# Layer 0 of a four-layer network: the wide votes' products as two operations, a new table of order, and half of the last tile's sums on VectorE

## The chip, the cores and the metric

The kernel runs on one core of a Trainium2 chip. The metric is the device time in microseconds (us) of one execution of the whole program, all four layers. Before the change the median of three runs is 6118.41 us (6118.16 to 6120.99). The engines are TensorE (PE in the profile; its weight loads are listed as PEld), VectorE (DVE), ScalarE (ACT), GpSimd (POOL) and SyncE (SP, which only issues DMAs here).

## The reference

The input `x` has shape (8, 16, 256, 256), all in float32. Four layers follow each other, each adding a function of the group-normalized input to its input. Only layer 0 is touched. It is a 3 by 3 convolution without bias whose 128 output channels are read as 8 capsules ("atoms") of 16 channels; the 8 images of the batch are the inputs between which the softmax is taken:

```
votes = conv(x, w).reshape(n, atoms, cout, h, wdt)
logits = zeros((a, b, d, e))
for _ in range(3):
    r = softmax(logits, axis=0)                       # over the 8 images
    preds = einsum('abcde,abde->bcde', votes, r)
    preds = squash(preds, axis=0)
    logits = logits + einsum('abcde,bcde->abde', votes, preds)
x = x + preds
```

`squash` scales by n2/((1+n2)·norm), where n2 is the sum of squares along the axis. In the first round the softmax is uniform, so that `preds` is a mean over the images.

## The kernel before

Layer 0 works on 64 tiles of four image rows (`TILES = H // 4`). A tile has two halves (`h` = 0 and 1) of two rows each. For each tile, `work(i)` (L505) writes down the operations:

- `prepare` (for tile i+2): fetch of `xs`, two products with `wd` that subtract means and normalize (`pd`, L487), a move on ACT (L490), and a DMA on ACT's queue that puts the rows into the scratch `d0` (L499).
- **Votes.** Half 0 goes through `votes(h, j)`, once for each row j: three fetches (`kt` in two parts, `kr`), four products with 32 rows of weights (L557), four with 128 rows (L550), two moves on ACT (L572). Half 1 goes through `wide(h)`: two fetches of 516 KB, then four calls of `votes_wide` (L579), one for each row j and each half g of the images. A call has two products with 128 rows (L587) and two with 64 rows (L591), all in one operation, and then a move on ACT (L596).
- **Squash** (L633), three times a tile: squares on ACT (L641), sums by eight small products `n` (L645), then a chain of small operations on ACT (L659 to L661), DVE (L665, L666), ACT (L670, L671) and POOL (L675 to L678) that ends in the factor `f`.
- **Logits** (L708), twice a tile: the factor is spread by four small products into `fb` (L697), DVE scales (L715) and multiplies with the votes (`pr`, L723, 2048 and 1536 elements), PE sums into `pl` (L733), ACT copies (L755 or L766), and POOL adds the older logits the second time (L760).
- **Softmax** (L771): transposes on PE (L780, L804), DVE and ACT between them.
- **Weighted** (L816), twice a tile: PE spreads the shares into `rb` and `r` (L831), DVE multiplies with the votes into `dd` (L842: per half three of 1024 elements and one of 512), and POOL adds the eight images up (L851: per half three of 512 and two of 1024 elements).
- The end: `fb` again, DVE scales (L893), POOL adds the input `res` (L896), ACT measures mean and square for the next layer (L908), SP stores.

The order in which all tiles' operations are issued is a fixed list made when the program is built. `_Order.run` (L258) ranks an operation of tile n at `n * period + TIMES[m]`, with a period of 48 and one number of `TIMES` for each operation of a tile. It always takes the lowest rank among those whose inputs exist and for which buffers are free. What is taken is appended to the queue of its engine; the engines then run their queues in order, and wait for each other by semaphores. The cost argument of `op` and its `mode` do not enter here: they belong to the search that made `TIMES`. Buffers limit how far tiles overlap: six `v` (three tiles), four `dd`, two `pr`, two `kt`, one `io` for `xs` and `res` together, and in PSUM three of `x` (for `pd`, `cv`, `fb`, `rb`) and two of `u` (for `n`, `pl`, `lg`, `rt`, `r`).

PE is used in four shapes in this layer: 128 rows by 128 columns of weights (L487, L550, L587, L780, L804), 64 rows (L591, L697), 32 rows (L557, L831), and 128 rows by 32 columns (L645, L733).

Of the kernel before, what the change touches and what calls it, by code (L numbers as in the profile page):

```python
# [12 lines left out]
ALU = mybir.AluOpType  # L13
# [10 lines left out]
TILES = H // 4  # L24
# [160 lines left out]
class _Buf:  # L185
# [10 lines left out]


TIMES = [
    -1017.19, 743.46, 708.62, 498.18, -984.65, -996.51, -997.22, 751.01, 751.99, 751.01, 752.12, 750.77,
    -967.35, -903.62, -974.59, 753.99, 754.00, 753.77, 445.66, 393.73, -780.66, -960.80, 755.37, 755.59, 760.20,  # L200
    707.64, 775.69, 780.13, 782.25, 565.91, 658.76, 763.54, 681.24, 605.08, 709.84, 767.15, 644.09, 776.33,
    664.78, 790.04, 756.59, 796.59, 757.08, 765.74, 797.09, 318.31, 799.87, 800.80, 377.30, 696.72, 800.88,
    717.59, 571.56, 737.04, 802.63, 604.46, 530.71, 804.53, 784.88, 636.95, 657.50, 800.06, 517.07, 807.24,
    715.03, 742.15, 830.33, 840.65, 809.85, 812.29, 605.85, 802.98, 816.03, 807.95, 821.83, 824.88, 831.28,
    830.39, 840.66, 789.85, 845.72, 805.49, 748.11, 612.37, 736.06, 636.75, 809.44, 848.88, 838.39, 852.49,
    854.69, 850.98, 859.07, 855.18, 468.16, 857.49, 859.83, 859.02, 698.63, 610.89, 868.22, 704.59, 653.78,
    580.88, 884.00, 654.67, 695.12, 888.80, 889.83, 889.82, 808.47, 890.27, 690.66, 805.44, 696.48, 782.31,
    896.59, 899.53, 896.48, 777.07, 667.15, 682.59, 886.03, 640.00, 674.37, 898.75, 899.76, 887.82, 843.57,
    670.73, 902.64, 828.29, 828.95, 658.08, 885.55, 571.52, 801.95, -872.70, 907.37, 403.39, 814.67, 908.69,
    735.69, 919.60, 844.76, 829.08, -789.01  # L210
]


# [79 lines left out]
class _Net:  # L293
# [123 lines left out]
    def layer0(self, wd, bd, less0, tiles=range(TILES)):  # L417
# [5 lines left out]
        nc, tc = self.nc, self.tc  # L423
        xf = self.d["x"].rearrange("b c h w -> (b c) (h w)")
        last = B - 1
        with ExitStack() as st:
# [6 lines left out]
            w = w0[:, : 2 * P].rearrange("p (s m) -> p s m", s=2)  # L433
# [12 lines left out]
            for i in range(2):  # L446
                t = one.tile([P, 4, WP], F32, name=f"dn{i}")
                nc.vector.memset(t, 0.0)
                ring.append(t)
            for row in (0, H + 1):  # L450
                nc.sync.dma_start(
                    out=self.d0[row * ROW : row * ROW + ROW].rearrange("(p w) -> p w", p=P), in_=ring[0][:, 0, :]
                )
                nc.sync.dma_start(
                    out=self.x1[row and 15, :, :, row and 9, row and 1, :].rearrange("b c w -> (b c) w"),
# [3 lines left out]
                    out=self.x1p[:, row and 1, :, row and H // 2, :], in_=ring[0][:, 0, 0:W]  # L459
# [7 lines left out]
            def buf(kind, shape, name=None):  # L467
                pool = psum if kind in banks else sbuf
                n = {**places, **banks}[kind]
                return _Buf(kind, lambda: pool.tile(shape, F32, name=name or kind, tag=kind, bufs=n))  # L470
# [34 lines left out]
            def work(i):  # L505
# [3 lines left out]
                def op(*a, **k):  # L509
                    ops.append(order.op(*a, **k))  # L510
# [7 lines left out]
                v = [buf("v", [P, 8, 512]) for _ in range(2)]  # L518
# [60 lines left out]
                def votes_wide(h, kt, j, g):  # L579

                    ps = buf("x", [P, 2, 512], "cv")

                    def products():
                        t = kt().rearrange("p (a w) -> p a w", a=8)
                        for n in range(2):
                            a = 4 * g + 2 * n
                            nc.tensor.matmul(ps()[:, n], w2[:, 0, j, :], t[:, a : a + 2, 0:W], start=True, stop=False)  # L587
                        for n in range(2):
                            a = 4 * g + 2 * n
                            at = slice(n * 64, n * 64 + 64)  # L590
                            nc.tensor.matmul(  # L591
                                ps()[:, n], w2[at, 1, j, :], t[at, a : a + 2, 2 - n : 2 - n + W], start=False, stop=True
                            )

                    def move():
                        nc.scalar.copy(  # L596
                            v[h]()[:, 4 * g : 4 * g + 4, j * W : j * W + W],
                            ps().rearrange("p n (a w) -> p (n a) w", w=W),
                        )

                    op("PE", 3.2, products, [(kt, 0), (kt, 1)], [(ps, 0), (v[h], "turn")], mode="votes")
                    op("ACT", 1.1, move, [(ps, 0)], [(v[h], g, j)])

                def wide(h):
                    kt = buf("kt", [P, 8 * WP])
                    for dx in range(2):

                        def fetch(dx=dx):
                            at = (4 * i + 2 * h) * ROW + dx
                            nc.sync.dma_start(  # L610
                                out=kt()[dx * 64 : dx * 64 + 64],
                                in_=self.d0[at : at + 4 * ROW].rearrange("(p f) -> p f", f=8 * WP),
                            )

                        op("SP", 0.5, fetch, [("d0", i), ("d0", i + 2 * h - 1)], [(kt, dx)], lag=6.0)
                    for g in (1, 0):
                        for j in range(2):
                            votes_wide(h, kt, j, g)

                def voted(h, a):  # L620
                    return [(v[h], a // 4, 0), (v[h], a // 4, 1)]
# [8 lines left out]
                def rows(ap):  # L630
                    return ap.rearrange("p (r w) -> p r w", w=W)
# [184 lines left out]
                def weighted(rs):  # L816


                    s = buf("s", [P, 2, 2, W])
                    for h in range(2):  # L820

                        def term(images, h=h):

                            rb = [buf("x", [P, 2, 512], "rb") if len(a) == 2 else buf("u", [P, 1, 512], "r6") for a in images]

                            def products():
                                for pair, r in zip(images, rb):
                                    for n, a in enumerate(pair):
                                        g, j = a // 4, (0, 2, 1, 3)[a % 4]
                                        at = slice(32 * j, 32 * j + 32)  # L830
                                        nc.tensor.matmul(  # L831
                                            r()[:, n], spread[at, g, h, :], rs()[at], start=True, stop=True
                                        )

                            op("PE", 1.25, products, [(rs, 0)], [(r, 0) for r in rb] + [(s, "turn")], mode="r32")
                            out = []
                            for pair, r in zip(images, rb):
                                n, a = len(pair), pair[0]
                                dd = buf("dd", [P, 2, 512])

                                def multiply(n=n, a=a, r=r, dd=dd):
                                    nc.vector.scalar_tensor_tensor(  # L842
                                        dd()[:, :n], r()[:, :n], 1.0 / B, v[h]()[:, a : a + n], ALU.subtract, ALU.mult
                                    )

                                op("DVE", 0.2 + 0.52 * n, multiply, [(r, 0)] + voted(h, a), [(dd, 0)])
                                out.append(dd)
                            return out

                        def add(out, a, b, us):  # L850
                            op("POOL", us, lambda: nc.gpsimd.tensor_tensor(out[0](), a[0](), b[0](), ALU.add),  # L851
                               a[1] + b[1], out[1])

                        d45, d6 = term([(4, 5), (6,)])
                        sh = (lambda h=h: s()[:, :, h], [(s, h)])
                        add(
                            sh,
                            (lambda h=h: rows(v[h]()[:, last]), voted(h, last)),
                            (lambda d=d6: rows(d()[:, 0]), [(d6, 0)]),
                            1.3,  # L860
                        )
                        d01, d23 = term([(0, 1), (2, 3)])
                        both = (d01, [(d01, 0)])
                        add(both, both, (d45, [(d45, 0)]), 2.4)
                        add(both, both, (d23, [(d23, 0)]), 2.4)
                        for n in range(2):
                            add(sh, sh, (lambda d=d01, n=n: rows(d()[:, n]), [(d01, 0)]), 1.3)
                    return s
# [7 lines left out]
                for _ in range(2):  # L876
                    ls = logits(s, read, f, before)
                    before = ls
                    t = weighted(softmax(ls))
# [1043 lines left out]
```

## Time and profile before

| what | value |
|---|---|
| median of three runs | 6118.41 us |
| profiled execution | 6118.06 us, span of its instructions 6116.3 us |
| layer 0, from the first `pd` product to the start of its closing statistics | 101.0 to 3275.8 us |
| from one place in a tile to the same place in the next, in the steady part | 47.59 us |
| PE busy, whole span | 5816.4 us (95%) |
| DVE, POOL, ACT busy, whole span | 85%, 63%, 53% |

In these tables a float32 product of 512 columns shows as two records of PE, and a transpose as one. A line of the timeline has a start, the busy time from first start to last end, the engine, the line of the code, the operation, its output and inputs, the sizes, and the count. A line of the chain of waits has a start, a length and what it is; the chain is followed back from the last instruction to whatever released it. "issue" in the chain is time in which nothing that the profile shows was waited for.

### The profile page before, as it was taken

The page shows a single profiled execution, that of the slowest core. Times are in us where ns is not written, and L with a number is a line of the kernel's source. Part 1 is how long each engine was busy: PE and PEld are TensorE (multiplying, and loading weights), DVE is VectorE, ACT ScalarE, POOL GpSimd, SP SyncE. Part 2 cuts the span into 40 slices and gives each one's busy share as a digit, 9 for nine tenths or more (in the row PEclk, how much of TensorE's full clock was granted, in tenths as well). Part 3 has the DMA queues.
Part 4 walks back from the last instruction along what each step waited for, and adds up shares of the span by engine and source line. Part 5 has one row for each costly group of instructions (what it writes and reads, how often), then busy time and mean ns, then how long its engine had stood idle before and what let it go on. Part 6 is the DMA issues. An engine that isn't in the chain of part 4 may idle for free.

```text
span 6116.3 us, 118361 instructions
## 1 busy us (share of the span) xinstructions
PE 5816.4 (95%) x46024; PEld 2945.8 (48%) x46024; DVE 5191.8 (85%) x6933; ACT 3236.8 (53%) x4986; POOL 3828.0 (63%) x3679
## 2 busy tenths in 40 slices
PE   2999999999999999999985999999999999999998
PEld 0344444444444444444432444444444589999853
DVE  5799999999999999999986999999999777777741
ACT  0444454444544445444435888888888533333321
POOL 0588888888888888888884444444443344444333
PEclk9999999999999999999997999999999999999999
DMA  7455555555555555555524555555556554445458
GB/s 291 114 141 136 128 138 143 137 136 128 143 141 136 132 131 144 141 136 129 136 75 132 186 184 179 181 179 179 181 182 177 155 101 102 96 89 103 115 179 265
DMA packets 599967, 902.55 MB, mean 148 GB/s; under 512 B 294130, under 2 KB 370514, under 8 KB 572402
## 3 DMA queue, kind: packets, MB, share of 16 engines
q1 hardware_dynamic: 555570, 831.70, 50.3%
q10 hardware_dynamic: 33984, 34.08, 1.8%
q0 software_dynamic: 9856, 29.20, 1.7%
q8 instruction: 367, 6.01, 0.4%
q14 instruction: 190, 1.56, 0.1%
HBM read 684.09 MB, written 210.77 MB: 146 GB/s over the span
## 4 chain that ended last, share of the span: by engine, by line
PE 80%; DVE 7%; issue 5%; POOL 4%; DMA 2%; ACT 2%; SPq 0%; DVEq 0%; POOLq 0%; ACTq 0%
PE ps L1123 23%; PE rb L831 8%; PE cv L587 7%; PE pq L1539 6%; PE pl L733 6%; PE cv L591 4%; PE cv L550 4%; PE psc L1607 4%; PE po L1623 4%; PE p L1740 3%; PE pv L1539 3%; DVE pr L723 2%; PE fb L697 2%; PE pd L487 2%; PE cv L557 1%
## 5 line engine op out<-in xcount | busy, mean ns | idle before, releaser
L1123 PE MATMUL ps<-bases,tw 128*32 128x512 f32 (+1 forms) x13824 | 1340.5, 545 | 13.3 <-POOL bases L1089 13.3
L851 POOL TENSOR_TENSOR dd<-dd 128x1024 f32<-128x1024 f32 x512 | 1212.0, 2367 | 70.0 <-DVE dd L842 64.8
L723 DVE TENSOR_TENSOR pr<-v,fb 128x2048 f32<-128x2048 f32 (+1 forms) x512 | 1020.7, 2014 | 17.0 <-PE pl L733 12.5
L1123 PEld LDWEIGHTS ps<-bases,tw 128*32 128x32 f32 x13824 | 620.4, 109 | 753.6 <-issue 477.3
L842 DVE SCALAR_TENSOR_TENSOR dd<-rb,v 128x1024 f32<-128x1024 f32 x768 | 906.7, 1214 | 8.8 <-POOL dd L851 3.3
L851 POOL TENSOR_TENSOR s<-s,dd 128x512 f32<-128x512 f32 x512 | 647.7, 1275 | 15.1
L1089 POOL TENSOR_TENSOR bases<-e,a 128x1024 f32<-128x1024 f32 (+1 forms) x264 | 615.9, 2354 | 12.5 <-DVE e L1082 12.2
L831 PE MATMUL rb<-rs,ct_fold 32*128 32x512 f32 x3072 | 593.0, 634 | 25.6 <-DVE pr L723 20.1
L1093 POOL COPY mark<-e 128x1 f32<-128x1 f32 x127 | 23.6, 186 | 865.3 <-DVE e L1061 857.4
L851 POOL TENSOR_TENSOR s<-v,dd 128x512 f32<-128x512 f32 x256 | 329.0, 1285 | 290.5 <-DVE dd L842 290.5
L587 PE MATMUL cv<-kt,w 128*128 128x512 f32 x1024 | 497.3, 608 | 11.8 <-DMA kt<-d 10.6
L733 PE MATMUL pl<-pr,ct_fold 128*32 128x512 f32 x3584 | 505.1, 601 | 3.0 <-DVE pr L723 3.0
L550 PE MATMUL cv<-kt,w 128*128 128x512 f32 x1024 | 477.3, 609 | 4.8 <-DMA kt<-d 4.8
L596 ACT COPY v<-cv 128x1024 f32<-128x1024 f32 x256 | 251.9, 1008 | 303.8 <-PE cv L591 303.8
L1637 POOL COPY y<-y 128x2 f32<-128x2 f32 x128 | 24.1, 189 | 599.5 <-DVE y L1628 599.5
L831 PEld LDWEIGHTS rb<-rs,ct_fold 32*128 32x128 f32 x3072 | 226.1, 185 | 325.3 <-issue 129.0
L697 PEld LDWEIGHTS fb<-f,ct_fold 64*128 64x128 f32 x3072 | 208.2, 188 | 310.2 <-issue 176.2
L1069 ACT ACTIVATE sq<-a 128x1024 f32<-128x1024 f32 (+1 forms) x264 | 263.9, 999 | 148.1 <-DVE a L1061 142.1
L842 DVE SCALAR_TENSOR_TENSOR dd<-r,v 128x512 f32<-128x512 f32 x256 | 177.0, 692 | 190.5 <-PE r L831 175.9
L572 ACT COPY v<-cv 128x1024 f32<-128x1024 f32 x256 | 258.2, 1009 | 139.2 <-PE cv L550 139.1
L550 PEld LDWEIGHTS cv<-kt,w 128*128 128x128 f32 x1024 | 184.7, 190 | 289.8 <-issue 283.0
L1082 DVE TENSOR_TENSOR a<-a,sq 128x1024 f32<-128x1024 f32 (+1 forms) x264 | 313.6, 1188 | 9.4 <-ACT sq L1069 9.4
(323 smaller groups left out, 11753.9 us busy)
## 6 DMA issues: line engine op xcount, KB each, us to landing
kt<-d SPq DMA_DIRECT2D x256, 387.0 KB
kt<-d SPq DMA_DIRECT2D x128, 516.0 KB
xr<-x1p SPq DMA_DIRECT2D x128, 512.0 KB
xt<-x1p SPq DMA_DIRECT2D x120, 512.0 KB
d<-dn ACTq DMA_DIRECT2D x64, 516.0 KB
kr<-d SPq DMA_DIRECT2D x128, 258.0 KB
kt<-d SPq DMA_DIRECT2D x128, 258.0 KB
x<-y SPq DMA_DIRECT2D x128, 258.0 KB
```

The source lines that it names most:

```text
L550: nc.tensor.matmul(ps[g]()[:, n], w[:, 0], t[:, a : a + 2, 0:W], start=False, stop=True)
L587: nc.tensor.matmul(ps()[:, n], w2[:, 0, j, :], t[:, a : a + 2, 0:W], start=True, stop=False)
L697: nc.tensor.matmul(fb()[:, j, n * P : n * P + P], unfold[at, h, n, :], f()[at, 3], start=True, stop=True,)
L723: nc.vector.tensor_tensor(pr()[:, :n].rearrange("p n (r w) -> p n r w", w=W), v[h]()[:, 4 * g : 4 * g + n].rearrange("p n (r w) -> p n r w ...
L733: nc.tensor.matmul(pl()[at : at + 32], sel[:, g, h, :], pr()[:, t, :], start=h == 0 and g == 0, stop=h == 1 and (g == 1 or t == 3),)
L831: nc.tensor.matmul(r()[:, n], spread[at, g, h, :], rs()[at], start=True, stop=True)
L842: nc.vector.scalar_tensor_tensor(dd()[:, :n], r()[:, :n], 1.0 / B, v[h]()[:, a : a + n], ALU.subtract, ALU.mult)
L851: op("POOL", us, lambda: nc.gpsimd.tensor_tensor(out[0](), a[0](), b[0](), ALU.add), a[1] + b[1], out[1])
L1082: nc.vector.tensor_tensor(q, q, part[4 + k], ALU.mult)
L1089: nc.gpsimd.tensor_tensor(ring[n % 3][:, 0, p : p + m, 1 : 1 + W], rows(e), rows(a), ALU.subtract)
L1123: nc.tensor.matmul(out if k is None else out[:, k], lhs, rhs, start=start, stop=stop, skip_group_check=True)
L1539: nc.tensor.matmul(out, lhs, rhs, start=start, stop=stop, skip_group_check=True)
```

## The change

It has three parts. `products()` of `votes_wide` becomes two operations, `most` (the two products with 128 rows) and `rest` (the two with 64 rows), each placed by the order on its own. `TIMES` has one number more for each of the four wide calls of a tile, and all its numbers are new. In the last tile (`i == TILES - 1`) the ten additions of half 1 (five in each of the two weighted sums) go to DVE; all others stay on POOL. The amount of arithmetic is the same.

```diff
@@ -196,18 +196,19 @@
 TIMES = [
-    -1017.19, 743.46, 708.62, 498.18, -984.65, -996.51, -997.22, 751.01, 751.99, 751.01, 752.12, 750.77,
...
+    788.93, 1208.48, 1101.33, 1188.73, -10349.17, -10412.56, -10390.23, 1181.37, 1174.54, 1141.94, 1180.94,
...
 ]
@@ -580,11 +581,14 @@
                     ps = buf("x", [P, 2, 512], "cv")
 
-                    def products():
+                    def most():
                         t = kt().rearrange("p (a w) -> p a w", a=8)
                         for n in range(2):
                             a = 4 * g + 2 * n
                             nc.tensor.matmul(ps()[:, n], w2[:, 0, j, :], t[:, a : a + 2, 0:W], start=True, stop=False)
+
+                    def rest():
+                        t = kt().rearrange("p (a w) -> p a w", a=8)
                         for n in range(2):
                             a = 4 * g + 2 * n
                             at = slice(n * 64, n * 64 + 64)
@@ -598,7 +602,8 @@
-                    op("PE", 3.2, products, [(kt, 0), (kt, 1)], [(ps, 0), (v[h], "turn")], mode="votes")
+                    op("PE", 1.8, most, [(kt, 0), (kt, 1)], [(ps, 0), (v[h], "turn")], mode="votes")
+                    op("PE", 1.0, rest, [(kt, 0), (kt, 1)], [(ps, 0)], mode="r64")
                     op("ACT", 1.1, move, [(ps, 0)], [(v[h], g, j)])
@@ -847,8 +852,10 @@
-                        def add(out, a, b, us):
-                            op("POOL", us, lambda: nc.gpsimd.tensor_tensor(out[0](), a[0](), b[0](), ALU.add),
+                        name, engine = ("DVE", nc.vector) if h and i == TILES - 1 else ("POOL", nc.gpsimd)
+
+                        def add(out, a, b, us, name=name, engine=engine):
+                            op(name, us, lambda: engine.tensor_tensor(out[0](), a[0](), b[0](), ALU.add),
                                a[1] + b[1], out[1])
```

## The prediction

> **What bounds the kernel now.** I read the busy time by stretches first: what limits layer 0, and where that stops.
>
> ```profile
> core 0: us, PE busy (x) PEld busy (x) DVE busy (x) ACT busy (x) POOL busy (x), PEclk, DMA share, GB/s
> 1973.00:2020.60 47.60, 46.91 (x294) 19.39 (x293) 43.38 (x48) 23.44 (x44) 42.16 (x36) 1.00 0.54 136
> 3164.00:3290.00 126.00, 56.71 (x334) 24.30 (x334) 70.03 (x107) 31.08 (x68) 81.14 (x73) 0.65 0.20 64
> ```
>
> In a steady tile (47.6 us) PE is busy 46.9, DVE 43.4, POOL 42.2: PE bounds, and two engines are 10% behind it, so that a short delay soon shows. In the tail (second row) no engine is full, POOL leads, and the granted clock is 0.65. Next the chain of waits inside one tile, for what a product, a change of shape and a wait cost:
>
> ```profile
> 2029.76 3.63 PE cv L550 x8
> 2033.39 0.60 PE rt L804 x4
> 2033.99 1.72 PE cv L587 x4
> 2035.71 1.06 PE cv L591 x4
> ...
> 2039.06 0.57 PE n L645 x16
> 2039.64 0.86 PE pl L733 x8
> 2040.49 0.65 PE fb L697 x8
> 2041.14 1.91 PE cv L587 x4
> ...
> 2047.89 0.69 DVE s L893
> 2048.66 1.27 POOL s L896
> 2049.93 1.24 POOL ls L760
> ```
>
> Four records of L587 take 1.72 after `rt`, which has their shape: 0.43 each. After `fb` (64 rows) they take 1.91, and L550 takes 3.63 for eight where 3.44 is due: **a change to a shape of 128 columns costs 0.19 to 0.20.** `n` and `pl` share a shape, so `pl` is 0.86 clean; `n` is 0.57 for 0.44 of work, so a change to 32 columns costs 0.13. The last rows are a wait: PE's `lg` stands behind POOL's `ls`, which stands behind an addition of the input. Then the tail, on POOL:
>
> ```profile
> 3247.17 4.77 POOL L851 TENSOR_TENSOR dd<-dd 128x1024 f32<-128x1024 f32 x2 [0.99 <-DVE dd L842]
> 3251.90 1.26 POOL L851 TENSOR_TENSOR s<-v,dd 128x512 f32<-128x512 f32 x1
> 3260.29 2.60 POOL L851 TENSOR_TENSOR s<-s,dd 128x512 f32<-128x512 f32 x2
> ```
>
> The last tile's last sums keep POOL busy without a break from 3247.17 to 3262.89, and layer 0 ends on them.
>
> **Steady part: work of PE.** Write F for 128x128, H for 64 rows, Q for 32 rows, C for 32 columns. From one `pd` to the next, PE's old order is F Q C H C Q F Q C H F Q F H Q C H F H Q C H C H Q F H F H: 29 changes, 6 of them to C. The changed program has F H F H Q H C Q F Q C H F Q F C H F H C Q C Q C F H F Q C: 29 again, 7 to C. So the split saves no change of shape: three of the four wide calls stay in one piece, and in the fourth the transposes `rt` (F) stand between the parts. 1 x (0.195 - 0.13) is a gain of 0.07. All products are the same: 36 full passes (15.5), 8 pairs of 64-row passes (3.4), 32-row groups (1.7 for votes, 6.9 for `rb`), `pl` 6.9, the small ones 5.7, together 40.1; with 23 x 0.195 + 6 x 0.13 = 5.3 this is 45.4 of the 47.59. **The other 2.2 are waits**, and they decide.
>
> **Steady part: waits.** I laid both orders out side by side over a tile, each instruction with the duration of its row (DVE: `pr` 2.28 and 1.75, `dd` 1.21 and 0.69, 0.08 less when the next follows at once; POOL: 2.37, 1.28, four steps of `f` 1.66; ACT: move 1.01, square 0.63), and with the gaps that the rows show between an end and what waits for it (0.05 to PE, 0.2 from PE's last start plus 0.43, 0.08 between dependent additions on POOL). For the old order that gives these waits of PE: second pair of `rb` 0.42 and 0.39 (bank still read by DVE's `pr` or `dd`), `rb` after L550 0.36, `lg` on ACT's copy 0.13, second pair of L557 0.24, `rt` and the product after it 0.22, `rb` 0.10, `lg` on POOL's `ls` 0.39, small ones 0.06: 2.31, which with the work comes within 0.1 of the measured 47.59. For the new order:
>
> - Gone: `lg` on `ls` (0.39), one of the two `rb` waits (0.4), `rt` (0.2), `rb` (0.1): 1.1.
> - Kept: `rb` after L550 0.38, `lg` 0.13, L557 0.24: the same.
> - **Second pair of `rb`, 0.65 in place of 0.42.** It needs the bank of `fb`. From the start of that `fb`: 0.76 to the scale, 0.69, then `pr` 2.28 and 1.75, 5.55 with the gaps. On PE only `fb`, `rt`, one wide call and half the `rb` lie between, 4.9.
> - **Second half of `n`, 0.36, new.** A 64-row half, then `lg`, four `rb` and half of `n` on PE, 2.05; against 0.2, the move 0.91, squares 0.53 and 0.63, 0.05 on ACT, 2.32; plus the weights that are then loaded in the open.
> - **`fb` on `f`, 0.28, new.** POOL has two additions of `dd`, three of `s` and the four steps of `f` in a row before it; dependent ones follow at 0.08 apart instead of overlapping by 0.04.
> - **A wide call on a bank of `dd` 0.26, `fb` on a bank of `pr` 0.20, small ones 0.10**, all new.
>
> The sum is 0.75 + 0.65 + 0.36 + 0.28 + 0.26 + 0.20 + 0.10 = 2.60. So a tile changes by 2.60 - 2.31 - 0.07 = **+0.22 to +0.24**; over some 60 tiles after the start and before the tail, **+14**. Bounds: each of the new waits is known to perhaps 0.05, and the old order was missed by up to 0.1; from 0 a tile (the lost waits outweigh: 0) to +0.42 (+25). If POOL's run of additions had more cover, `fb` would not wait; if it has less, what is late next is DVE's `pr`, then the `rb` behind it.
>
> **Fetches.** The number of DMAs is the same. In the trace a `kt` lands 6.3 to 6.6 after issue (up to 9.1), and PE waited for one in only 9 cases, 6.8 in all. The new order has the same two `kt` buffers to fetch ahead into. 0, bounds -4 to +7.
>
> **Start.** SP's queue now has tile 1's `xs` behind eight fetches of tile 0's votes, which wait for `d0` (landed at 110.1). They carry 2.6 MB, 11 us at the 239 GB/s that the stretch from 113 to 129 us shows: `xs` lands near 125 to 128, and PE, where `pd` of tile 1 stands ahead of the votes, waits for it (before: votes at 120.1). But the wide products could not start before 147.5 anyhow, since their fetch took 15.8 beside others; the later one finds fewer beside it (6.6 in the steady part). +1, bounds -4 to +8.
>
> **Tail.** Half 1's additions, 2 x 1.21 + 3 x 0.69 = 4.5 on DVE by layer 1's sums of that shape and `s`-sized rows, run beside half 0's 8.6 on POOL. The last sums would end near 3258 instead of 3262.9, and those of the round before gain about 3. Against it: on ACT the four measuring operations of tile 62 (0.8 each) now stand ahead of the inverse of tile 63's last squash, and wait for tile 62's last addition: +4. Together **-3**, bounds -8 to +3.
>
> Here a rule speaks against the change. The layer 1 rows first:
>
> ```profile
> 4003.66 1.21 DVE L1082 TENSOR_TENSOR a<-a,sq 128x1024 f32<-128x1024 f32 x1
> 4004.79 1.21 DVE L1082 TENSOR_TENSOR e<-e,sq 128x1024 f32<-128x1024 f32 x1
> 4005.92 1.21 DVE L1082 TENSOR_TENSOR a<-a,sq 128x1024 f32<-128x1024 f32 x1
> 4004.02 4.76 POOL L1089 TENSOR_TENSOR bases<-e,a 128x1024 f32<-128x1024 f32 x2
> ```
>
> DVE's operations with two inputs in SBUF run at 1.13 steps beside two POOL additions of 2.38, and neither is held up. The Trainium skill (SBUF — State Buffer, "SBUF: two separate sides") says that such a DVE operation and a GpSimd one take a shared port pair for a whole instruction, the other being blocked. By that rule the moved 9.0 of DVE's additions would queue with POOL's and the tail would end near 0 instead of -3.
>
> **Sum.** 6118.06 (span 6116.3 and 1.8 around it) + 14 + 0 + 1 - 3 = 6130; the median of the runs lies 0.35 above the profiled one. **I forecast 6130 us**, 0.19% above the median. 0.2% (12.2 us) is also about what a measurement of this kernel can tell from no change, so the forecast sits just short of that line, and I give both sides of it nearly the same chance.
>
> **Rivals.**
>
> - *The exchange of waits is even* (same): the new waits are covered as the lost ones were. For it: counts of shapes and products are equal, and each wait is only some tenths. Against it: dependent additions of POOL now stand in a row. Time 6118 + 0 + 1 - 3 = 6116; a chance of 0.17.
> - *POOL becomes the loop* (slower): POOL's run from `dd` to `f` gates `fb`, `fb` gates `pr`, and `pr` gates the next `dd`. POOL's 42.2 busy of 47.6 speaks against it; no pause longer than 2.2 in the new layout speaks for it. From another 0.2 late per tile on it decides: 60 x 0.42 - 2, 6141. 0.15.
> - *The split pays* (faster): of the new waits only the kept 0.75 and the 0.65 appear, 1.4 instead of 2.60; 60 x (1.4 - 2.31 - 0.07) = -59, 6057; already 0.3 a tile less than before decides it (6098). Against it: each new wait has a chain by rows. 0.06.
> - *Start lost* (slower): the late `xs` pushes all by 8 while the rest holds: 6138. 0.05.
>
> **Numbers.** The forecast's own case, 6124 to 6137, has the remaining 0.57. The range 6115 to 6143 leaves out the split that pays and the outer ends of the two slower rivals. Slower by over 0.2%: 0.15 + 0.05 + half of the forecast's case (rounded up, for what the layout misses mostly adds), 0.50; same 0.17 + the other half, 0.44; faster 0.06.
>
> **What would show it.** The distance from one `pd` to the next in the steady part: 47.8 (47.59 before). PE's waits there: `n` on ACT's squares, `fb` on POOL's `f`, `rb` on DVE's `pr` by 0.6, and no `lg` on `ls`. First L588 at 146 to 150. In the tail, L676 after the measuring of tile 62, and DVE's additions at 0.69 and 1.21 beside POOL's. A distance of 47.6 or less makes the prediction wrong, and above 48.0 POOL's rival right.

## The result, and the profile after

The changed kernel takes 6141.57 us (median of six runs, 6136.62 to 6143.91) against 6118.51 of the kernel before (six runs, 6113.98 to 6123.82). The ratio is 1.0036, with a 95% interval of 1.0026 to 1.0046: 23 us slower, on the side that was forecast, and near the upper end of the range of 6115 to 6143. The prediction had 12 us.

The two profiled executions show where the time went. The first wide product of a tile (L587 before, L588 after) serves as a mark. The end of layer 0 is taken here as the end of the last ScalarE operation of its closing statistics (L338 before), 3.9 us behind their start that the table of before has:

| | before | after | difference |
|---|---|---|---|
| start of tile 0's first wide product | 147.5 | 151.2 | +3.7 |
| the same of tile 5 | 368.2 | 369.1 | +0.9 |
| from one tile to the next, steady | 47.59 | 47.94 | +0.35 |
| the same of tile 60 | 2986.1 | 3006.1 | +20.1 |
| from there to the end of layer 0 | 293.6 | 295.1 | +1.5 |
| end of layer 0 | 3279.6 | 3301.3 | +21.6 |
| rest of the span | 2836.6 | 2839.5 | +2.9 |

The last row is not the change's doing: the layers behind took between 2831.2 and 2845.7 in the twelve profiles of this study that leave them alone, for one and the same code. So layer 0 lost 21.6 us, and 19.2 of them between tile 5 and tile 60. One steady tile of the changed kernel, in the view by stretches (columns as in the prediction):

```profile
core 0: us, PE busy (x) PEld busy (x) DVE busy (x) ACT busy (x) POOL busy (x), PEclk, DMA share, GB/s
2015.32:2063.26 47.94, 46.77 (x297) 18.89 (x293) 43.49 (x47) 23.56 (x45) 42.33 (x36) 1.00 0.53 136
```

The work is the same within 0.2 on every engine but for PE's weight loads, which have 0.5 less, and PE even has 0.14 less than the 46.91 of before. What grew is the time in which PE stands: 0.7 before, 1.2 after. For which releaser, the view of waits tells; here PE's largest over layer 0, first of the kernel before:

```profile
engine line waited for: us in total, times, longest us
...
PE lg L780 <- POOL ls L760: 22.4, 64, 1.5
PE rb L831 <- DVE pr L723: 20.1, 62, 1.0
```

and of the changed one:

```profile
PE rb L836 <- DVE pr L728: 45.1, 123, 0.6
...
PE pd L488 <- DMA xs<-in_x_dram: 24.6, 1, 24.6
...
PE cv L588 <- DVE dd L847: 10.9, 62, 0.2
```

A wait with some 60 occurrences is one of each tile; one with few, as the 24.6 for `xs`, belongs to the start or the tail. Before, each tile has `lg` on POOL's `ls` and one `rb` on DVE's `pr`. After, the first is gone, `rb` on `pr` comes twice a tile and costs 25.0 more, and a wide call on the bank that `dd` reads is new with 10.9. The view lists only time in which nothing of PE runs; two more waits show in the timeline of the same tile, as groups that are longer than their work:

```profile
2025.68 1.14 PE L836 MATMUL rb<-rs,ct_fold 32*128 32x512 f32 x8 [0.45 <-DVE pr L728]
...
2034.73 0.70 PE L836 MATMUL rb<-rs,ct_fold 32*128 32x512 f32 x2 [0.28 <-DVE pr L728]
...
2044.83 1.07 PE L738 MATMUL pl<-pr,ct_fold 128*32 128x512 f32 x8
2046.02 1.16 PE L702 MATMUL fb<-f,ct_fold 64*128 64x128 f32 x16
...
2057.70 1.98 PE L588 MATMUL cv<-kt,w 128*128 128x512 f32 x4 [0.18 <-DVE dd L847]
...
2062.38 0.95 PE L650 MATMUL n<-sq,ct_fold 128*32 128x128 f32 x16
```

In the tile of before, the same groups in the same view:

```profile
2038.99 0.65 PE L645 MATMUL n<-sq,ct_fold 128*32 128x128 f32 x16
2039.45 1.04 PE L733 MATMUL pl<-pr,ct_fold 128*32 128x512 f32 x8
2040.43 0.71 PE L697 MATMUL fb<-f,ct_fold 64*128 64x128 f32 x8
```

The last row of after is `n` with its second half late: 0.95, where the same sixteen records are 0.65 long before. That is the wait on ACT's squares, 0.30. Between the rows of 2044.83 and 2046.02 lie 1.19, where the step from `pl` to `fb` is 0.98 before: `fb` on the bank of `pr`, 0.21.

In the tail, the additions of half 1 on DVE stand beside POOL's (two sorts of rows from the timeline, in order of time):

```profile
3210.52 4.79 POOL L858 TENSOR_TENSOR dd<-dd 128x1024 f32<-128x1024 f32 x2 [0.42 <-DVE dd L847]
3213.73 2.13 DVE L858 TENSOR_TENSOR s<-v,dd 128x512 f32<-128x512 f32 x1
3215.39 2.94 POOL L858 TENSOR_TENSOR s<-s,dd 128x512 f32<-128x512 f32 x2
...
3223.92 1.42 DVE L858 TENSOR_TENSOR s<-s,dd 128x512 f32<-128x512 f32 x2
...
3267.91 5.10 POOL L858 TENSOR_TENSOR dd<-dd 128x1024 f32<-128x1024 f32 x2
3269.50 1.31 DVE L858 TENSOR_TENSOR s<-v,dd 128x512 f32<-128x512 f32 x1
3273.09 3.56 POOL L858 TENSOR_TENSOR s<-s,dd 128x512 f32<-128x512 f32 x2
3274.30 1.22 DVE L858 TENSOR_TENSOR dd<-dd 128x1024 f32<-128x1024 f32 x1
```

With POOL idle an addition of 512 elements takes DVE 0.69 (two of them 1.42, at 3223.92). Beside POOL's it took 2.13: from 3213.73 to 3215.86, while POOL's second addition ended at 3215.31. The one at 3269.50 took 1.31 and ended 0.55 behind the end of a POOL addition too: of the pair at 3267.91 the first ended at 3270.26. In turn POOL's rows are longer: 5.10 for two that take 4.79 elsewhere, 3.56 for two that take 2.62. So here one engine waits until the other's instruction is over. DVE's `dd` products, of which one input lies in PSUM (`rb`), aren't held up beside the same additions: the one from 3211.49 to 3212.70, inside the pair at 3210.52, took its usual 1.22.

### The profile page after: what moved, and what is told of

Same layout as the page of the kernel before. It is cut to its first block, busy times and chain, and to the rows that moved or that the text cites. A ratio compares the mean times of both kernels' runs of the same rounds, so it can differ in the third digit from the quotient of the medians.

```text
span 6140.8 us, 118472 instructions
## 1 busy us (share of the span) xinstructions
PE 5803.9 (95%) x46024; PEld 2919.8 (48%) x46024; DVE 5209.6 (85%) x6943; ACT 3243.6 (53%) x4986; POOL 3824.2 (62%) x3669
## 4 chain that ended last, share of the span: by engine, by line
PE 73%; DVE 15%; issue 4%; ACT 3%; DMA 3%; POOL 1%; SPq 0%; DVEq 0%; POOLq 0%; ACTq 0%
PE ps L1130 22%; DVE pr L728 6%; PE pq L1546 6%; PE pl L738 6%; PE cv L588 6%; DVE dd L847 4%; PE rb L836 4%; PE cv L551 4%; PE psc L1614 4%; PE po L1630 4%; PE cv L595 3%; PE pv L1546 3%; PE p L1747 3%; PE fb L702 2%; PE pd L488 2%
## 5 line engine op out<-in xcount | busy, mean ns | idle before, releaser
L858 POOL TENSOR_TENSOR dd<-dd 128x1024 f32<-128x1024 f32 x508 | 1201.6, 2365 | 44.5 <-DVE dd L847 24.6
L836 PE MATMUL rb<-rs,ct_fold 32*128 32x512 f32 x3072 | 554.7, 634 | 47.5 <-DVE pr L728 45.1
L588 PE MATMUL cv<-kt,w 128*128 128x512 f32 x1024 | 497.8, 608 | 19.5 <-DVE dd L847 10.9
L836 PEld LDWEIGHTS rb<-rs,ct_fold 32*128 32x128 f32 x3072 | 183.8, 185 | 328.5 <-issue 138.9
L1089 DVE TENSOR_TENSOR a<-a,sq 128x1024 f32<-128x1024 f32 (+1 forms) x264 | 314.7, 1192 | 9.9 <-ACT sq L1076 9.9
L1089 DVE TENSOR_TENSOR e<-e,sq 128x1024 f32<-128x1024 f32 (+1 forms) x264 | 314.7, 1192 | 1.8 <-ACT sq L1076 1.8
```

The costliest lines, as they stand in the source:

```text
L836: nc.tensor.matmul(r()[:, n], spread[at, g, h, :], rs()[at], start=True, stop=True)
L858: op(name, us, lambda: engine.tensor_tensor(out[0](), a[0](), b[0](), ALU.add), a[1] + b[1], out[1])
L1089: nc.vector.tensor_tensor(q, q, part[4 + k], ALU.mult)
```

## The experiments

But for the two runs on layer 1, every kernel here has `most` and `rest` as two operations, with the table that is named. "t60" is the start of tile 60's first wide product. Each time is compared with the kernel before on the same chip. The three runs on the tail for which no whole time is given were executed once each.

The distance from t60 to the end of layer 0 hangs on more than the edit. In the tail the clock that is granted to TensorE falls to half for some us at a time, and not at the same places in every execution. Four profiles with the same code in layer 0 (before, the split alone, and the two runs on layer 1) have 293.6, 293.6, 293.6 and 296.8. In the last of them the clock between 60 and 110 us after tile 63's first wide product is 0.69 in the mean, in the others 0.76, and PE's products there are longer. So a difference of up to 3 us from t60 isn't the edit's before the clock has been compared.

**The split alone.** The old table, with each `rest` ranked as its `most`, all additions on POOL:

```diff
-    -960.80, 755.37, 755.59, 760.20, 707.64, 775.69, 780.13, 782.25, 565.91,
+    -960.80, 755.37, 755.37, 755.59, 760.20, 760.20, 707.64, 775.69, 775.69, 780.13, 782.25, 782.25, 565.91,
```

> The two operations most and rest, but with the old table: each rest has the number of its most, so it follows it at once, and all additions stay on POOL. My theory (the split by itself costs and saves nothing; the new list of waits makes the loss): 47.59 us from one first wide product to the next, layer 0 as before, 6118 +-4. Rival (the split costs: a bank that is held between two operations, or one more wait): above 47.7 a tile, over 6125. Rival (the split pays by itself): below 47.5.

Measured: 47.59 a tile, 6117.43, ratio 0.9998 (0.9989 to 1.0007). Two operations instead of one cost nothing and bring nothing; both rivals fall.

**The new order without the parting.** Each `rest` gets the number of its `most`. In the steady order only one call was parted, by `rt`:

```diff
-    1186.83, 1189.99, 1155.77, 1199.21, 1194.70, 1165.26, 1211.22, 1169.54, 1016.54, 1216.82, 1080.34,
+    1186.83, 1186.83, 1155.77, 1199.21, 1199.21, 1165.26, 1211.22, 1211.22, 1016.54, 1216.82, 1216.82,
```

> The changed kernel with each rest ranked like its most, so that the transposes rt no longer stand between the parts of the fourth wide call; the rest of the new table stays. My theory (parting them is the one place where the split is used, and the new order needs it because VectorE's share has to reach the softmax's way back): about +0.4 a tile over the changed kernel, 48.2 to 48.4 a tile, 6160 to 6170. Rival (the parting costs a change of shape and is itself the loss): below 47.9, back towards 47.6, 6122. Rival (it does nothing): 47.93, 6141.

Measured: 48.31 a tile, 6169.42, ratio 1.0085 (1.0068 to 1.0102). The parting is worth 0.37 a tile in the new order. So the split is used, and the loss lies in the rest of the order.

**POOL's part in the steady tile.** In the changed kernel, the two last additions of each weighted sum on one row of two:

```diff
-    add(sh, sh, (lambda d=d01, n=n: rows(d()[:, n]), [(d01, 0)]), 1.3)
+    add(sh0, sh0, (lambda d=d01, n=n: rows(d()[:, n])[:, 0:1], [(d01, 0)]), 0.7)    # sh0: s()[:, 0:1, h]
```

> The changed kernel with the two last additions of each weighted sum (s<-s,dd, two a half) done on one row of two only: half of each such addition is left out, eight of 1.28 become about 0.7 per tile, 4.6 us of POOL's 42 a tile. My theory (POOL only delays the one fb that waits for its factor f, by about 0.28): 47.6 to 47.7 a tile, 16 to 20 us of the whole, 6123 +-4. Rival (POOL is the loop of the tile): the tile falls by 1 us or more, to 46.9 or less, 6080 or less. Rival (POOL has no part in it): 47.93 and only the tail is shorter, 6137.

Measured: 47.66 a tile, 6117.83. POOL had 4.2 us less to do in a tile (38.10 in place of 42.33), and the tile became 0.28 shorter. That is the wait of `fb` on POOL's `f`, and no more: from the start of the 64-row products in front of that `fb` to `rt` behind it, PE takes 1.51 in place of 1.78. POOL isn't the loop. The whole came out below 6119, and the tail is 6.0 shorter too (289.1 from t60).

```profile
2004.51:2052.17 47.66, 46.49 (x296) 18.97 (x293) 43.48 (x47) 23.37 (x45) 38.10 (x36) 1.00 0.53 136
```

The waits of `rb` on `pr` and of the wide call on `dd` are untouched (45.2 and 10.9 us over the layer).

**The wait that went.** In the old order, POOL's `ls` on half of its columns:

```diff
-    nc.gpsimd.tensor_tensor(ls(), ls(), more(), ALU.add)
+    nc.gpsimd.tensor_tensor(ls()[:, 0:256], ls()[:, 0:256], more()[:, 0:256], ALU.add)
```

> The old table with the old order (both parts of the wide call together, additions on POOL), and POOL's addition of the older logits (ls) done on half of its columns: the other half is left out. My theory (in the old order PE's transposes lg waited 0.39 a tile for this addition, a wait that the new order has not): 47.4 a tile in place of 47.59, 12 us of the whole, 6105. Rival (POOL has cover there, and PE waits for something else): 47.59, 6117. Rival (POOL is a loop that sets the tile): 0.6 less, 47.0, 6080.

Measured: 47.49 a tile, 6109.60, ratio 0.9986 (0.9976 to 0.9995). Half of what was expected. The wait itself is gone: of its 64 cases 2 are left in the list, and PE's step from that `rb` to `lg` fell from 1.54 to 1.15, by the 0.39 of the prediction. But then `fb` stands 0.18 longer (0.72 in place of 0.54), the next `rt` 0.04 and `pd` 0.10 (1.91 in place of 1.81), and only 0.10 is left. So three quarters of a wait that was removed came back in the next ones behind it.

**The tail with all additions on POOL.**

```diff
-    name, engine = ("DVE", nc.vector) if h and i == TILES - 1 else ("POOL", nc.gpsimd)
+    name, engine = ("POOL", nc.gpsimd)
```

> The changed kernel with all additions on POOL, also those of the last tile's second half. My theory: the steady part stays at 47.93; layer 0 ends 5 us later after the last tile's first wide product (156 to 157 us instead of 151.3), since VectorE's additions save about 5 and the measuring of tile 62 on ScalarE gives 3.5 back; 6146. Rival (VectorE's additions block those of POOL through a shared port, so nothing was won): 151 to 152, 6141. Rival (VectorE's additions themselves delay tile 62's end and cost): under 150, 6138.

Measured: 6146.16, 47.94 a tile; from tile 63's first wide product to the end 152.6 (after: 151.3), from t60 297.9 (after: 295.1). So with DVE's additions the tail is 1.2 to 2.8 shorter, not 5. The clock differs between the two profiles (it first falls 27 us ahead of tile 63's first wide product with all on POOL, 21 us behind it in the changed kernel), so that the sum can't be told closer; the next runs take it apart.

**DVE's additions in the last weighted sum only.**

```diff
-    name, engine = ("DVE", nc.vector) if h and i == TILES - 1 else ("POOL", nc.gpsimd)
+    name, engine = ("DVE", nc.vector) if h and final and i == TILES - 1 else ("POOL", nc.gpsimd)
```

> The changed kernel, with VectorE's additions only in the second weighted sum of the last tile; the five of the first one are back on POOL. My theory (in the first sum VectorE is still busy with other work, and its additions are held up by POOL's through their shared access to SBUF, 2.13 us for one of 0.69; this cost 1.4 to 2): from the first wide product of tile 60 to the end of layer 0 293 to 294 us in place of 295.1, and layer 0 ends 4 to 5 earlier than with all on POOL (297.9). Rival (the first sum's additions won 3 us as my prediction had it): 298. Rival (they did nothing): 295.

Measured: 293.6 from t60. This profile and the one with all additions on POOL (297.9) have the same course of the clock up to the last sum and reach its first `dd` 257.1 and 257.3 after t60: in the last sum DVE's additions save 4.3. Against the changed kernel, 1.5 less, the clock differs. But the next run has the changed kernel's additions and nearly the clock of this one: there tile 62's last sum, which follows tile 63's first, begins 2.1 later and tile 63's last sum 1.8 later (258.9 in place of 257.1). So in the first sum DVE's additions cost about 2.

**The measuring of tile 62, two runs.** The first one ranks it 60 later, the second 30, with the edit of the run above:

```diff
-    at = n * self.period + self.times[-m] if n else -1000.0 - m
+    at = n * self.period + self.times[-m] + (60.0 if n == len(sets) - 2 and m in (2, 3) else 0.0) if n else -1000.0 - m
```

> The changed kernel, with the two measuring operations of tile 62 ranked 60 later, so that on ScalarE they stand behind the inverse of tile 63's last squash. My theory (in the changed kernel this inverse stood 3.4 us behind the measuring, 3283.7 to 3287.1): from the first wide product of tile 60 to the end of layer 0 some 292 us in place of 295.1; the tile stays at 47.93; 6138. Rival (the residual of tile 63 arrives late anyhow, since its buffer is freed only by tile 62's last addition): 294.5 to 295.1.

Measured: 298.6 from t60: worse by 3.5. With 60, more than a period of 48, tile 62's measuring went behind that of tile 63, and the fetch of the next layer's constants (`ct_ident`) behind tile 63's stores in SP's queue. The inverse did come earlier (from the last eight `n` of PE to the `fb` that needs the inverse 4.3 us in place of 8.0), and it came to nothing. The edit was wrong, not yet the theory; so, with 30:

> The changed kernel with both repairs of its tail: VectorE's additions only in the last weighted sum, and the measuring of tile 62 ranked 30 later, behind the inverse of tile 63's last squash but, unlike in the run with 60, still ahead of tile 63's own measuring and with SyncE's queue in its old order. My theory (the inverse stood 3.4 behind the measuring): from the first wide product of tile 60 to the end of layer 0 290 to 291 us, where the changed kernel has 295.1 and the one with the first repair alone 293.6. Rival (the fetch of tile 63's residual ends late anyhow and takes the place of the wait): 293 to 293.6.

Measured: 290.7, 2.9 less than with the first repair alone. But 1.3 of them are the clock's. The run with the first repair alone had half the clock for 3.4 us ahead of tile 63 (3126.2 to 3129.6), this one had not; the same four records of a wide product, first there, then here:

```profile
3127.03 3.19 PE L588 MATMUL cv<-kt,w 128*128 128x512 f32 x4
```

```profile
3127.07 1.88 PE L588 MATMUL cv<-kt,w 128*128 128x512 f32 x4
```

At the first `dd` of the last sum, ahead of all that was moved, the new run leads by 1.3. Behind it the step from the last eight `n` to `fb`, in which the inverse lies, fell from 8.0 to 6.5. ACT in the tail of this kernel, from the timeline:

```profile
3284.98 0.72 ACT L916 ACTIVATE sq<-s,less 128x512 f32<-128x512 f32 x1
...
3285.70 0.29 ACT L675 ACTIVATE f<-f 128x128 f32<-128x128 f32 x1
...
3286.24 0.71 ACT L916 ACTIVATE sq<-s,less 128x512 f32<-128x512 f32 x1
...
3292.69 0.72 ACT L916 ACTIVATE sq<-s,less 128x512 f32<-128x512 f32 x1 [4.81 <-POOL s L904]
```

Only half 1's measuring (3286.24) went behind the inverse (L675); it now lies in time in which ACT waits anyhow, for the additions of tile 63 (4.81 before the last row). Half 0's still stands ahead. The theory holds for the half that was moved: 1.6 of its 3.4.

**What decides between the tail's additions and layer 1's products.** The prediction had set layer 1's rows against the rule that the tail then followed. Two runs change the kind of operation there:

```diff
-    nc.vector.tensor_tensor(q, q, part[4 + k], ALU.mult)
+    nc.vector.tensor_tensor(q, q, part[4 + k], ALU.add)
```

> The kernel before, with VectorE's two products of layer 1 (a<-a,sq and e<-e,sq, 256 of 128x1024 beside POOL's subtractions) changed to additions; the values of layer 1 are others. In the prediction these rows, 1.21 beside POOL's 2.38, stood against the rule of the shared access. The last tile's additions on VectorE were held up (0.69 became 2.13 and 1.31), the products are not. Theory (it is the kind of operation: additions on VectorE take the shared access, products do not): these rows grow beyond 1.21, some to 2.4 or more, POOL's rows beyond 2.4, and layer 1, which VectorE bounds over 90%, becomes longer by some 50 us or more. Rival (it is the place, the buffers, or POOL's own operation that differs): 1.21 as before, 6118.

Measured: 6120.64, ratio 1.0004 (0.9994 to 1.0014), DVE's rows at 1.21 as before. Then POOL's subtraction as well (`ALU.subtract` to `ALU.add` in L1089):

> The kernel before, with additions in layer 1 in place of VectorE's two products and of POOL's subtraction beside them; the values of layer 1 are others. VectorE's additions alone beside POOL's subtractions stayed at 1.21. Theory (it is POOL's addition, of which all blocking partners in the last tile were, that takes the shared access): VectorE's rows grow to 1.5 and more in the mean, POOL's beyond 2.4, layer 1 becomes 30 us or more longer. Rival (the kind of operation plays no part; the buffers' places or shapes decide): 1.21 and 2.39 as before, 6118.

Measured: 6120.52, ratio 1.0003 (0.9992 to 1.0014):

```profile
L1082 DVE TENSOR_TENSOR a<-a,sq x264: 411/1215/1224, 3297.1 to 4813.0; 128x1024 f32<-128x1024 f32 x128, 128x256 f32<-128x256 f32 x4
...
L1089 POOL TENSOR_TENSOR bases<-e,a x264: 729/2402/3309, 3300.0 to 4815.5; 128x1024 f32<-128x1024 f32 x128, 128x256 f32<-128x256 f32 x4
```

The three numbers behind the count are the shortest, the median and the longest in ns. Not one of these 256 large rows of DVE is held up, nor of the 256 with `e` (longest 1222), though the shape and the operation are those of the tail. The kind of operation is not it.

Both runs left alone what does differ. The kernel takes `sq` from PSUM (L1000 of before: `psum if kind == "sq" else sbuf`), so that these operations of DVE read one input from SBUF, and the tail's additions (`v`, `s`, `dd`) two. Layer 1 has another operation of DVE, L1101, with two inputs in SBUF (`xt` or `xr`, and `bases`). The trace of before shows it beside the same subtractions of POOL:

```profile
4007.05 1.21 DVE L1082 TENSOR_TENSOR e<-e,sq 128x1024 f32<-128x1024 f32 x1
4008.18 1.68 DVE L1101 SCALAR_TENSOR_TENSOR bases<-xt,xm,bases 128x1024 f32<-128x1024 f32 x1
4009.78 1.27 DVE L1101 SCALAR_TENSOR_TENSOR bases<-xr,xm,bases 128x1024 f32<-128x1024 f32 x1
...
4811.00 3.29 POOL L1089 TENSOR_TENSOR bases<-e,a 128x1024 f32<-128x1024 f32 x1 [0.18 <-DVE e L1082]
4811.97 3.41 DVE L1101 SCALAR_TENSOR_TENSOR bases<-xr,xm,bases 128x1024 f32<-128x1024 f32 x1
```

POOL's pair of 4004.02, which the prediction shows, ended at 4008.78. The row of 4007.05, with `sq` in PSUM, ran inside it at its 1.21; the one of 4008.18 took 1.68 and ended 1.08 behind POOL; the next, with POOL idle, took 1.27. Of the 256 large rows of L1101 all 126 that began inside an instruction of POOL ended 1.08 to 1.20 behind its end (median length 1.67), and the 130 others took 1.27 to 1.29. This isn't a wait for a result of POOL: in 125 of the 126, those with `xt`, that instruction writes another of the three buffers of `bases` than the one they read. In turn POOL's longest row (3.29, elsewhere 2.40) began while one of L1101 ran. So in this kernel, in the tail as in layer 1, DVE is held up where both its inputs lie in SBUF, and not where one lies in PSUM. That is read from rows; no run moved a buffer.

**A third table.** What the runs say can be used: the split is free, and in the old order PE's last two wide calls lie close together.

> A third table for the two operations, made from the old one by moving single numbers and laying each order out with the durations of the trace's rows; all additions on POOL. On PE it is the old order but for one place: the two most of the third and fourth wide call follow each other, then fb, then both rest, so that a tile has 27 changes of shape in place of 29 (two of 0.195 less), and the wait of lg on POOL's ls (0.39) is gone, for one of rb on DVE's that is 0.39 longer and small ones that are shorter by 0.2. My theory (work and waits decide, and the split pays where it brings products of one shape together): 47.0 to 47.2 a tile, 0.4 to 0.55 less than before, 25 to 32 us of the whole, 6088 to 6096. Rival (a wait that the layout doesn't have, of PE for a fetch or for a bank, takes it back): 47.6, 6118. Rival (only one of the two savings comes): 47.3 to 47.4, 6103.

Measured: 47.11 a tile, as expected; 6086.14, 2 below the expected range; ratio 0.9950 (0.9937 to 0.9962): faster than both kernels. PE's rows at the place, first before, then with the third table:

```profile
2051.70 1.88 PE L587 MATMUL cv<-kt,w 128*128 128x512 f32 x4
2053.52 1.13 PE L591 MATMUL cv<-kt,w 64*128 64x512 f32 x4
2054.48 0.61 PE L697 MATMUL fb<-f,ct_fold 64*128 64x128 f32 x8
2055.02 1.98 PE L587 MATMUL cv<-kt,w 128*128 128x512 f32 x4
...
2057.99 0.66 PE L804 MATMUL rt<-ct_fold,e 128*128 128x128 f32 x4
```

```profile
2029.24 3.60 PE L589 MATMUL cv<-kt,w 128*128 128x512 f32 x8
2032.77 0.71 PE L703 MATMUL fb<-f,ct_fold 64*128 64x128 f32 x8
2033.32 1.89 PE L596 MATMUL cv<-kt,w 64*128 64x512 f32 x8
2035.13 0.66 PE L810 MATMUL rt<-ct_fold,e 128*128 128x128 f32 x4
```

With both parts together, eight products of one shape follow each other (3.60 in one piece), and one change there and one back are gone. From the third call's start to `rt` it is 5.89 in place of the 6.29 of before (2051.70 to 2057.99): 0.40 of the 0.48 that the tile won. Of the 64 waits of `lg` for `ls` 3 are left in the list, and that `rb` waits longer by as much (from it to `lg` 1.55, 1.54 before): an even exchange.

> The same with VectorE's additions in the last weighted sum of the last tile alone. My theory: from the first wide product of tile 60 to the end of layer 0 some 4 us less than the same kernel with all on POOL (4.3 was the gain in the new order), the tile as there. In the whole time 4 us can hardly be told. Rival (the gain hung on the new order's tail): within 1 us.

Measured: 47.11 a tile, 6081.75, ratio 0.9943 (0.9930 to 0.9957); from t60 291.7 in place of 293.5: 1.8, between the two readings. The sum itself, from its first `dd` to the second square, fell from 19.2 to 16.0, 3.2 less and near the theory's 4, but it began 1.5 later. That is the clock's doing too: in this execution it fell to half at 3124.1, 9 us earlier behind tile 63's first wide product than in the other, and records of `pl` there took 1.06 in place of 0.62. One of its DVE additions took 2.21 beside POOL's. Between the two kernels' whole times the intervals overlap.

## Why the prediction was right, and where it was not

- **Bound.** PE sets the tile, and the shapes and products are the same: right. PE's busy time fell by 0.14 a tile where one change of shape less into 128 columns was to bring 0.07.
- **The split saves no change of shape:** right for this order, and by itself it costs and brings nothing (47.59 with the old order). But the price of a change, 0.195, is right too, and with the third table the split does save two. The rival of the split that pays was given 0.3 to 1.0 a tile by lost waits; it took another order, and came by shapes.
- **The waits.** Each of the named ones is there. `fb` on `f`: 0.28, measured 0.28 by cutting POOL's additions. `n` on the squares: 0.36, measured 0.30 (0.95 for 0.65). `fb` on the bank of `pr`: 0.20, measured 0.21. The wide call on `dd`: 0.26, of which the list of waits shows 0.18. The lost `lg` on `ls`: 0.39, measured 0.39 in that place. "Second pair of `rb`, 0.65 in place of 0.42" is 0.73 by PE's steps (2.65 from that `rb` to the next `fb`, where the same group takes 1.92 at the other place). These errors are small and of both signs. What failed is a size, the 2.31 and 45.4 for the old order. The prediction's own parts (products, changes of shape, waits) give 40.1 + 5.20 + 2.60 = 47.90 for the new one, where 47.94 was measured, but 40.1 + 5.27 + 2.31 = 47.68 for the old one, where 47.59 was known. It saw that its old order was off by up to 0.1, left this in the bounds, and took the difference of the two layouts, 0.22 to 0.24; the new layout against the measured 47.59 would have given 0.31 of the 0.35. Which of the old order's terms is too large, no run shows. Over 60 tiles this and the rest of the 0.12 are 7 us of the 11.6 that were missing; some 3 are the tail's.
- **POOL as the loop, the even exchange:** neither. 47.94 lies near the 48.0 that was to prove POOL's rival right, but the run that took 4.2 us of POOL's work away gave 0.28 back.
- **Fetches.** PE waited for a `kt` once in layer 0 of the changed kernel, at its start (8.6), and in no tile behind it: 0, as forecast. (The nine cases and 6.8 us of the prediction are those of PE's weight loads; its products have none between 200 and 3000 us before either.)
- **Start.** The mechanism is there: PE's `pd` of tile 1 waits 24.6 for `xs`, in one piece, and the first wide product comes at 151.2, just outside the 146 to 150. It is caught up: +0.9 at tile 5, for +1 forecast. Other executions lie at 365.6 to 368.2 with the old order and at 368.9 to 371.2 with the new one there, so that it may be up to +3.
- **Tail.** Forecast -3, measured about +0.5 (1.5 from t60, of which three steady tiles explain 1.0), with the clock's spread of up to 3 upon it. The terms can be told better than their sum. The measuring ahead of the inverse was to cost 4: the step from the last eight `n` to `fb` is 8.0 in place of the 4.3 of before, 3.7. The last sum was to gain 4.9, and gained 4.3. The step that failed is "those of the round before gain about 3": they cost about 2. There DVE is still in the middle of tile 63's softmax and of tile 62's end, so that the additions stand in its queue ahead of work that PE waits for, and one of them was held up by POOL for 1.4.
- **The rule.** The Trainium skill (SBUF — State Buffer, "SBUF: two separate sides") says that a DVE operation with two inputs in SBUF and a GpSimd operation take a shared port pair for a whole instruction, the other being blocked. The prediction set this aside for rows of layer 1 that it read as "operations with two inputs in SBUF". They are not: `sq` lies in PSUM. So these rows never spoke against the rule, and the rows of this case agree with it: in the tail DVE's addition ran on for 0.55 after POOL's had ended, twice (3215.31 to 3215.86, 3270.26 to 3270.81), POOL's was 0.94 longer when DVE was first, and in layer 1 all 126 rows of L1101 that met POOL were held up. That the prediction's sum by the rule, a tail near 0, came nearer than its -3 is luck for the most part: the rule was to take away the gain of the moved additions by their queueing, but the last sum kept 4.3 of its 4.9, and what the tail lost, it lost in the round before.

## What to carry to other kernels

When an engine bounds a loop and its work stays the same, lay the two orders out instruction by instruction and count the waits on both sides: the balance of nine waits of 0.1 to 0.65 gave two thirds of the loss, and its sign. Set the new layout against the time that was measured, and not against a layout of the old order that is known to be off. A wait is worth its length only until the next one behind it; here three quarters of one that was removed came back at once, while a change of shape that was saved stayed saved. Work moved to an idle engine in a tail pays where that engine has nothing else to do, and an end that is then earlier must not stand behind another tile's bookkeeping in some queue. Before a row is called to speak against a rule, look up in the kernel where its operands lie. And compare two tails only where their clocks agree.

## What the runs showed of the hardware

- An operation of DVE with both inputs in SBUF and one of POOL block each other for a whole instruction: in the tail (0.69 became 2.13 and 1.31, and 2.21 with the third table; POOL's pair of 2.62 became 3.56) and in layer 1 (L1101, 1.28 became 1.67 in the median of 126 rows, some 48 us of DVE's time in all; one of POOL's 2.40 became 3.29). With one input in PSUM DVE's operations on 128x1024 run beside POOL's at 1.21.
- In the tail the granted clock falls to half for stretches of 3.4 us and more (a wide product of 1.88 took 3.19), not at the same places in every execution, and the same code of layer 0 took 293.6 to 296.8 from t60.
- The layers behind layer 0 vary by 14.5 us between executions with the same code (2831.2 to 2845.7), more than most effects here. The distance from tile to tile repeats to 0.02 (47.94 to 47.96 in five kernels with the new order), and carries what a median of runs can't.
